# A spectral and mixture-of-experts kernel: column products, gate, spectrum and schedule rearranged

## The chip, the cores and the metric

The kernel runs on one core of one Trainium2 chip. The metric is the device time of one execution in microseconds (us); a comparison takes the median of several executions. TensorE (PE) multiplies matrices into PSUM; VectorE (DVE), ScalarE (ACT) and GpSimd (POOL) work on tiles; SyncE (SP) issues most transfers. Each engine runs its own instructions in order, and engines wait for each other with semaphores. The order within an engine is fixed when the kernel is built, by a scheduler that may move instructions against the order of the Python text.

## The reference: what is computed

The input x has 16 images, 64 channels, 128x128 pixels, float32. Layer 0 is a spectral convolution with a Hartley transform, 20x20 modes, followed by Gaussian blurs over all four axes and a column mask. Layer 1 is a group norm, a Fourier block on 32x32 modes, a second group norm and a mixture of experts:

```
x_ht = dht_2d(x);  out_ht[:, :, :20, :20] = compl_mul2d(x_ht[:, :, :20, :20], w1)
y    = gaussian_smoothing_4d(dht_2d(out_ht) / (H*W)) * mask
h    = afno(group_norm(y)) + y            # afno adds its own input again
feats = gelu(fe_w @ group_norm(h) + fe_b)
out  = sum over 2 shared of gelu(shared_w @ feats + b) / 2
gate_w = softmax of the 4 largest of 16 scores / 2, from the mean of feats
out += sum over experts of gelu(expert_w @ feats + b) * gate_w;   out + h
```

## The kernel before

Everything is float32. The image between the layers is never formed: it stays as 400 mode coefficients, and the pixels are made only once, late.

**Forward stage (L184 to L247), one image after the other.** The image is loaded in four pieces `xt` of 16 channels (1 MB each, five buffers). For each 8 channels, 16 small products with `fwd1` (L202) make a PSUM tile `ps`, which is copied into `t1`, by ScalarE and VectorE in turn (L207, L209). Then 40 column products with `fwd2` (L221) make the 20x20 modes; ScalarE copies half of them to `pn` (L224), VectorE combines them into `xm` (L228 to L231) and adds them, with the weights of the blur over images, into `x2` for up to nine images (L241, L243). When an image of `x2` is complete, VectorE writes a negated and a copied half (L246, L247). With the first eleven images come the weights `wk`: half of them straight, half in reversed order of the second mode, read so from memory (L214).

**Mode mixing (L249 to L285).** For each of 11 rows of modes, 20 products of `wk` with `x2` (L261), copied to `om` by both engines; then a blur over channels (L277) gives `ot`, 400 modes in four chunks of 100 partitions.

**Group norm and mode products (L288 to L448).** `group_norm(h)` runs for two halves of eight images: `dev` products (L340, 4x4), squares on ScalarE (L342), means (L346) and sums (L349), then a chain of VectorE instructions that ends with the scales `s1p`, the shifts `shp` and `sh`. Then for each image, 16 products `psx` with `spec` (L434), scaled by VectorE (L438), and one image-half behind them the first layer of the Fourier block (L419) with a Gelu (L421), written to memory as `o1d`. For ten of the images, `modes` picks 40 coefficients of all images (L401) into `ok`, which goes to memory as `od` and `ond`.

**Stage 5 (L453 to L847), one period per image.** Its constants are loaded first (L463 to L491). The pieces of an image are:

- `spectrum` (L549): loads `s` and the mode part of `bm`.
- `spectrum_f` (twice, L560): second layer of the Fourier block, 64 products into one PSUM tile; VectorE adds the bias `b2` on the way to `bm` (L578) and at the end the shift `sh` (L582).
- `rows` (eight, L588): inverse transform along one axis, `bm` to `u`.
- `pixels` (eight, L613): inverse along the other axis, `u` times `inv2` over 105 rows, copied by ScalarE to `h` (L632), with VectorE's statistics behind it (L636).
- `norm2` (three steps, L645): second group norm, folded into the weights `fs` and a bias.
- `feature` (eight, L677): features, Gelu on ScalarE (L691).
- `gate` (eight steps, L697): small products and activations, the 16 scores ranked on all 128 partitions, and four gathers of expert weights `wl` (L764).
- `group` (48, L812): one product of a tile of features with one shared or chosen expert (L784), Gelu on ScalarE (L789), and VectorE's weighted addition into `h` (L792). After its last one the tile is stored (L803).

All large pieces share three PSUM tiles `pe`. `h` has 14 tiles, eight of them per image, `f` nine, `g` seven. `PIECES` gives each piece its position, counted in groups of its own image; the pieces of all images are sorted by position, so that one image's groups lie beside the preparation of the next:

```
(spectrum_f, (-53, -49)),
(feature, (-9, -9, -8, -7, -6, -6, -3, -1)),
(step("norm", norm2), (-20, -18, -14)),
(step("gate", gate), (2, 3, 4, 6, 7, 7, 8, 10)),
(rows, (-48, -48, -41, -40, -40, -39, -38, -38)),
(pixels, (-36, -33, -28, -24, -24, -24, -24, -24)),
(group, range(NG)),
```

An evacuation by ScalarE is put into its queue one piece later (`on_act`), an addition by VectorE one more after that (`on_dve`).

Of the kernel before, what the change touches and what calls it, by code (L numbers as in the profile page):

```python
# [11 lines left out]
F32 = mybir.dt.float32  # L12
# [17 lines left out]
HR, KC = 52, 105  # L30
CL = C // 2
# [22 lines left out]
def constant_tables():  # L54
# [23 lines left out]
    inv1, inv2 = np.zeros((128, 2, N)), np.zeros((KC, N))  # L78
# [7 lines left out]
    inv1 = inv1.reshape(128, 2, 2, N // 2).transpose(0, 1, 3, 2).reshape(128, 2 * N)  # L86
# [27 lines left out]
    spec = spec.swapaxes(2, 3).reshape(NM, MD * MD) / N  # L114
    spec = np.stack([spec.real, spec.imag], 1)
    dev = np.linalg.qr(dev.reshape(41 * 42, NM), mode="r") / N
# [6 lines left out]
    for loc in range(5):  # L123
# [5 lines left out]
    lower = np.broadcast_to((f_ < e_).reshape(1, NE * NE), (128, NE * NE))  # L129
    ranks = np.broadcast_to(np.repeat(np.arange(TOPK), NE)[None], (128, TOPK * NE))  # L130
# [4 lines left out]
        "inv2": inv2,  # L135
        "spec": chunked(spec.reshape(NM, 2 * MD * MD)),
        "dev": chunked(dev.T.copy()),
        "mean": chunked(np.repeat(mean.reshape(NM, 1), 128, 1)),
        "blurc": blur_matrix(C).T * 2.0 ** -14,
        "sel": sel.reshape(CH, 5 * 32),  # L140
        "grp": grp,
        "lower": lower,
        "ranks": ranks,
        "ident": half[:, None] == np.arange(C)[None, :],
        "eidx": 64 * np.arange(NE)[None, :] + half[:, None],
# [5 lines left out]
def hartley_afno_moe_kernel(ctx: ExitStack, tc: tile.TileContext, a: dict, out: bass.AP):  # L151
# [15 lines left out]
    otp = on_modes.enter_context(tc.tile_pool(name="ot", bufs=1))  # L167
# [4 lines left out]
    sh = const.tile([P, NB, CL], F32, name="sh")  # L172
# [4 lines left out]
    with tc.tile_pool(name="modes", bufs=1) as mp:  # L177
# [6 lines left out]
        with tc.tile_pool(name="f_x", bufs=5) as xp, tc.tile_pool(name="f_t", bufs=2) as tp, \  # L184
# [4 lines left out]
            fwd2 = load(fc, "fwd2", [P, 2 * K, W1], nc.gpsimd)  # L189
            seen = set()  # L190
            for b in range(NB):

                t1 = tp.tile([P, 2 * K, C], F32, name="t1")
                for c0 in range(0, C, 16):
                    xt = xp.tile([P, 16, N], F32, name="xt")
                    nc.sync.dma_start(xt, a["x"][b, :, c0:c0 + 16])
                    for g in range(2):
                        ps = pp1.tile([P, 8, W1], F32, name="ps1")
                        for i in range(8):
                            for h in range(2):  # L200
                                cols = slice(h * 64, (h + 1) * 64)
                                nc.tensor.matmul(ps[cols, i, :], lhsT=xt[:, g * 8 + i, cols],  # L202
                                                 rhs=fwd1, start=True, stop=True)
                        cs = slice(c0 + g * 8, c0 + g * 8 + 8)
                        src = ps[:, :, 0:2 * K].rearrange("p c j -> p j c")
                        if g:
                            nc.vector.tensor_copy(t1[:, :, cs], src)  # L207
                        else:
                            nc.scalar.copy(t1[:, :, cs], src)  # L209
                if b <= K // 2:  # L210
                    nc.sync.dma_start(wk[0:C, b], a["w"][b])
                    kn = (-b) % K
                    nc.sync.dma_start(wk[C:P, b, 0], a["w"][kn, :, 0])
                    nc.sync.dma_start(wk[C:P, b, 1:K], a["w"][kn, :, K - 1:0:-1])  # L214
# [18 lines left out]

                xf = xm.rearrange("p a b -> p (a b)")
                for bo in range(NB):
# [9 lines left out]
                    if not gb[bo, b + 1:].any():  # L245
                        nc.vector.tensor_scalar(x2[0:C, 1, bo], x2[C:P, 0, bo], -1.0, None, ALU.mult)  # L246
                        nc.vector.tensor_copy(x2[C:P, 1, bo], x2[0:C, 0, bo])  # L247

        with tc.tile_pool(name="m_o", bufs=1) as op, \  # L249
                tc.tile_pool(name="m_p", bufs=3, space=PSUM) as pp, \  # L250
                tc.tile_pool(name="m_p2", bufs=2, space=PSUM) as pp2:
            blurc = load(op, "blurc", [C, C], nc.gpsimd)
            om = op.tile([C, NB, NM], F32, name="om")
            omk = om.rearrange("o b (k2 k1) -> o k1 k2 b", k1=K)
            for k1 in range(K // 2 + 1):
# [9 lines left out]
                nc.scalar.copy(omk[:, k1, 0:K:2], lo[:, :, 0])  # L265
                nc.vector.tensor_copy(omk[:, k1, 1:K:2], up[:, :, 0])
                if k1 % (K // 2):
                    nc.scalar.copy(omk[:, K - k1, 0:1], lo[:, 0:1, 1])
                    nc.scalar.copy(omk[:, K - k1, K - 2:0:-2], lo[:, 1:, 1])
                    nc.vector.tensor_copy(omk[:, K - k1, K - 1::-2], up[:, :, 1])  # L270

            for b0 in range(0, NB, 8):
                for ch in range(4):
                    ps = pp2.tile([CH, 8, C], F32, name="pst")
                    for i in range(8):
                        for m0, m1 in ((0, C), (C, CH)):
                            nc.tensor.matmul(ps[m0:m1, i, :],  # L277
                                             lhsT=om[:, b0 + i, ch * CH + m0:ch * CH + m1],
                                             rhs=blurc, start=True, stop=True)
                    dst = ot[:, ch, b0 * C:(b0 + 8) * C]  # L280
                    src = ps.rearrange("p b c -> p (b c)")
                    if ch % 2:
                        nc.scalar.copy(dst, src)
                    else:
                        nc.vector.tensor_copy(dst, src)  # L285


    with tc.tile_pool(name="s_c", bufs=1) as sc, tc.tile_pool(name="s_w", bufs=2) as sw, \  # L288
# [102 lines left out]
        for h in range(2):  # L391
            group_norm(h)
# [525 lines left out]
```

## Time and profile before

| what | value |
|---|---|
| time, median of 3 | 1924.02 us (1912.71 to 1928.27) |
| profiled execution, span | 1919.1 us, clock 0.974 |
| forward stage, to the first mixing product | 268.75 us |
| mixing and channel blur | 268.75 to 294.9 us |
| group norm | 294.96 to 338.03 us |
| mode products and first layer | 338.03 to 496.3 us |
| changeover and first image's preparation | 496.3 to 572.5 us |
| 15 periods of stage 5 | 85.6 us each |

A line of a group or a timeline has the source line, the engine, the operation, what it writes and reads, how often, its busy time and mean, and in brackets or behind the bar the idle time ahead of it with what ended that. A line of the waits has the waiting instruction, the one it waited for, the sum in us, how often, and the longest. `PEld` is the load of weights into TensorE, `SPq` the queue of transfers that SyncE issues. In the line of 40 slices each digit is the busy share in tenths.

### The profile page before, as it was taken

The page shows a single profiled execution, that of the slowest core. Times are in us where ns is not written, and L with a number is a line of the kernel's source. Part 1 is how long each engine was busy: PE and PEld are TensorE (multiplying, and loading weights), DVE is VectorE, ACT ScalarE, POOL GpSimd, SP SyncE. Part 2 cuts the span into 40 slices and gives each one's busy share as a digit, 9 for nine tenths or more (in the row PEclk, how much of TensorE's full clock was granted, in tenths as well). Part 3 has the DMA queues.
Part 4 walks back from the last instruction along what each step waited for, and adds up shares of the span by engine and source line. Part 5 has one row for each costly group of instructions (what it writes and reads, how often), then busy time and mean ns, then how long its engine had stood idle before and what let it go on. Part 6 is the DMA issues. An engine that isn't in the chain of part 4 may idle for free.

```text
span 1919.1 us, 55574 instructions
## 1 busy us (share of the span) xinstructions
PE 1735.4 (90%) x24568; PEld 946.2 (49%) x24568; DVE 1399.6 (73%) x1999; ACT 1278.1 (67%) x1542; POOL 146.4 (8%) x143
## 2 busy tenths in 40 slices
PE   6776779999689999999999999999999999999987
PEld 6676774332355454454635454454535445453521
DVE  2354653421139898988889898988989898888988
ACT  1111121112258888888888988888888888888896
POOL 0000000003001011010101001010101101010110
PEclk9899999999889999999999999999999999999998
DMA  9999823014312223222321223223222322222023
GB/s 331 310 303 299 291 73 96 33 56 124 92 21 35 79 55 70 67 47 68 67 78 35 80 56 68 67 46 89 47 78 38 84 54 63 67 51 74 26 67 90
DMA packets 140626, 181.15 MB, mean 94 GB/s; under 512 B 107456, under 2 KB 108709, under 8 KB 131965
## 3 DMA queue, kind: packets, MB, share of 16 engines
q1 hardware_dynamic: 136512, 170.55, 32.1%
q0 software_dynamic: 3872, 7.04, 1.5%
q8 instruction: 193, 3.16, 0.7%
q14 instruction: 49, 0.39, 0.1%
HBM read 98.51 MB, written 79.04 MB: 93 GB/s over the span
## 4 chain that ended last, share of the span: by engine, by line
PE 45%; ACT 18%; DVE 17%; issue 15%; DMA 3%; SPq 1%; DVEq 0%; POOL 0%; ACTq 0%; POOLq 0%
PE pe L784 10%; DVE h L792 9%; ACT g L789 9%; PE pe L624 9%; PE psx L434 6%; PE ps L202 6%; PE pe L602 4%; ACT f L691 4%; PE ps L221 2%; DVE stats L636 2%; ACT u L607 2%; DVE bm L578 2%; PE pso L419 2%; PE psd L340 2%; DMA xt<-in_x_dram 2%
## 5 line engine op out<-in xcount | busy, mean ns | idle before, releaser
L792 DVE SCALAR_TENSOR_TENSOR h<-g,wt,h 128x1024 f32<-128x1024 f32 x512 | 623.9, 1278 | 59.7 <-ACT g L789 59.7
L789 ACT ACTIVATE g<-pe,wl 128x1024 f32<-128x1024 f32 x512 | 541.2, 1142 | 41.9 <-PE pe L784 40.4
L784 PE MATMUL pe<-f,wl 64*64 64x512 f32 x4096 | 492.8, 602 | 3.9 <-DMA wl<-exd,ati 3.6
L792 DVE SCALAR_TENSOR_TENSOR h<-g,h 128x1024 f32<-128x1024 f32 x256 | 302.7, 1219 | 52.7 <-ACT g L789 52.2
L789 ACT ACTIVATE g<-pe,vec_sb 128x1024 f32<-128x1024 f32 x256 | 279.6, 1134 | 7.5 <-PE pe L784 4.2
L784 PEld LDWEIGHTS pe<-f,wl 64*64 64x64 f32 x4096 | 137.9, 132 | 275.0 <-ACT g L789 119.6
L784 PE MATMUL pe<-f,shw 64*64 64x512 f32 x2048 | 259.9, 602 | 0.0
L624 PEld LDWEIGHTS pe<-inv_sb,u 105*128 105x128 f32 x2048 | 234.9, 193 | 50.4 <-ACT g L789 36.5
L624 PE MATMUL pe<-inv_sb,u 105*128 105x128 f32 x2048 | 246.5, 279 | 1.4 <-ACT u L607 1.4
L202 PE MATMUL ps<-fwd_sb,xt 128*64 128x64 f32 x4096 | 144.3, 237 | 52.7 <-issue 38.0
L636 DVE BATCH_NORM_STATS2 stats<-h 128x6 f32<-128x512 f32 x256 | 162.6, 683 | 35.1 <-ACT h L632 34.5
L632 ACT COPY h<-pe 128x1024 f32<-128x1024 f32 x128 | 129.6, 1012 | 78.2 <-PE pe L624 69.0
L691 ACT ACTIVATE f<-pe,fb 128x1024 f32<-128x1024 f32 x128 | 148.0, 1184 | 35.0 <-PE pe L687 35.0
L202 PEld LDWEIGHTS ps<-fwd_sb,xt 128*64 128x64 f32 x4096 | 139.6, 152 | 56.0 <-issue 44.1
L687 PE MATMUL pe<-h,fs 64*64 64x512 f32 x1024 | 140.9, 622 | 13.6 <-DVE bm L582 11.8
L607 ACT COPY u<-pe 105x1024 f32<-105x1024 f32 x128 | 125.5, 1033 | 36.2 <-PE pe L602 36.2
L602 PEld LDWEIGHTS pe<-inv_sb,bm 64*64 64x64 f32 (+1 forms) x4096 | 119.2, 123 | 53.3 <-PE pe L784 20.5
L602 PE MATMUL pe<-inv_sb,bm 64*64 64x128 f32 (+1 forms) x4096 | 135.2, 271 | 10.5 <-DVE gs L702 8.6
L209 ACT COPY t<-ps 128x320 f32<-128x320 f32 x64 | 27.3, 426 | 148.2 <-PE ps L202 148.2
L434 PE MATMUL psx<-spec_sb,ot 100*64 100x512 f32 x512 | 116.7, 598 | 0.0
L421 ACT ACTIVATE o<-pso,b 128x512 f32<-128x512 f32 x32 | 22.0, 687 | 121.5 <-PE pso L419 121.5
L784 PEld LDWEIGHTS pe<-f,shw 64*64 64x64 f32 x2048 | 67.7, 132 | 55.9 <-issue 22.5
(160 smaller groups left out, 1250.7 us busy)
## 6 DMA issues: line engine op xcount, KB each, us to landing
xt<-in_x_dram SPq DMA_DIRECT2D x64, 1024.0 KB
out_dram<-h SPq DMA_DIRECT2D x256, 256.0 KB
o1d<-o SPq DMA_DIRECT2D x16, 512.0 KB
s<-o1d SPq DMA_DIRECT2D x16, 512.0 KB
bm<-od SPq DMA_DIRECT2D x96, 50.0 KB
wk<-in_w_dram SPq DMA_DIRECT2D x11, 320.0 KB
wk<-in_w_dram SPq DMA_DIRECT2D x11, 304.0 KB
spec_sb<-in_spec_dram SPq DMA_DIRECT2D x1, 3200.0 KB
```

Source lines behind the costliest of these rows:

```text
L202: nc.tensor.matmul(ps[cols, i, :], lhsT=xt[:, g * 8 + i, cols], rhs=fwd1, start=True, stop=True)
L434: nc.tensor.matmul(ps[ri * C:(ri + 1) * C], lhsT=ot[:, kc, b * C:(b + 1) * C], rhs=spec[:, kc, ri * 1024 + n * 512:ri * 1024 + (n + 1) * 512],
L602: nc.tensor.matmul(ps[cs, h, i, :], lhsT=bm[rs, 4 * q + i, cs], rhs=inv1[rs, part], start=True, stop=True)
L607: nc.scalar.copy(dst.rearrange("p h s n -> p n h s"), ps[0:KC].rearrange("p h s n -> p n h s"))
L624: nc.tensor.matmul(ps[:, r // 4, r % 4 * N:(r % 4 + 1) * N], lhsT=box["u"][0:KC, 2 * row:2 * row + 2, :].rearrange("p h c -> p (h c)"), rh ...
L632: nc.scalar.copy(h, ps)
L636: nc.vector.bn_stats(box["stats"][:, 2 * t + p, :], h[:, p])
L687: nc.tensor.matmul(ps[p * C:(p + 1) * C, half], lhsT=box["fs"][rows_], rhs=box["h"][t][rows_, p], start=True, stop=True)
L691: nc.scalar.activation(f, ps, AF.Gelu, bias=box["fb"], accum_out=box["sums"][:, t:t + 1])
L784: nc.tensor.matmul(ps[half * C:(half + 1) * C, p], lhsT=w[rows_], rhs=f[rows_, half], start=True, stop=True)
L789: nc.scalar.activation(g, ps, AF.Gelu, bias=bias)
L792: nc.vector.scalar_tensor_tensor(h, g, share(), h, ALU.mult, ALU.add)
```

## The change

The change touches every stage.

- Forward: the column products are written one image behind the row products, all copies of `ps` are made by ScalarE, the negated half of `x2` too; the reversed half of `wk` is loaded straight into `wn` and reversed by ScalarE.
- Mixing: `om` is laid out over 128 partitions, the channel blur uses both row halves of the array, and four PSUM tiles.
- Constants are loaded earlier, on the other side of the memory, beside mixing and the mode products.
- Group norm: both halves side by side on 64 partitions each, `dev` as an upper triangle (10 products for 16), and the results as one small tile `gs1`.
- First layer: two products of 64 columns for one of 128.
- Bias and shift: the bias `b2` of the spectrum becomes two more rows of `u` and `inv2` (107 for 105), made once; the shift is the bias of ScalarE's copy to `h`. So the spectrum is copied by ScalarE, plainly, and VectorE leaves it.
- Gate: the 16 experts lie on 16 partitions; ranks and picks are 16x16, and a product with ones spreads the result over 128 partitions.
- Schedule: new positions.

```diff
+            wn = fc.tile([P, K, C], F32, name="wn")
+            def along_columns(b, t1):          # L221 to L247 of before
...
-                        nc.vector.tensor_scalar(x2[0:C, 1, bo], x2[C:P, 0, bo], -1.0, None, ALU.mult)
+                        nc.scalar.mul(x2[0:C, 1, bo], x2[C:P, 0, bo], -1.0)
...
-                        if g:
-                            nc.vector.tensor_copy(t1[:, :, cs], src)
-                        else:
-                            nc.scalar.copy(t1[:, :, cs], src)
+                        nc.scalar.copy(t1[:, :, cs], src)
+                    if c0 == 0 and behind:
+                        along_columns(*behind)
+                behind = (b, t1)
+                if 0 < b <= K // 2 + 1:
+                    k = b - 1
+                    nc.scalar.copy(wk[C:P, k, 0], wn[C:P, 0])
+                    nc.scalar.copy(wk[C:P, k, 1:K], wn[C:P, K - 1:0:-1])
                 if b <= K // 2:
                     nc.sync.dma_start(wk[0:C, b], a["w"][b])
-                    nc.sync.dma_start(wk[C:P, b, 0], a["w"][kn, :, 0])
-                    nc.sync.dma_start(wk[C:P, b, 1:K], a["w"][kn, :, K - 1:0:-1])
+                    nc.sync.dma_start(wn[C:P], a["w"][(-b) % K])
...
-            om = op.tile([C, NB, NM], F32, name="om")
+            om = op.tile([P, NB, NM // 2], F32, name="om")
...
+                    pq = [pp2.tile([CH, 8, C], F32, name="pst") for h in range(2)]
                     for i in range(8):
+                        for h, (m0, m1) in ((0, (0, C)), (1, (C, CH)), (1, (0, C)), (0, (C, CH))):
...
+        for g, cols in halves:
+            for rc in range(4):
+                for kc in range(rc, 4):
+                    nc.tensor.matmul(ps[:CH], lhsT=dev[:, kc, rc * CH:(rc + 1) * CH],
+                                     rhs=ot[:, kc, cols], start=(kc == rc), stop=(kc == 3))
...
-            nc.tensor.matmul(ps, lhsT=wc.rearrange("p r c -> p (r c)"), rhs=xk[:, cols],
-                             start=True, stop=True)
+            for ri in range(2):
+                nc.tensor.matmul(ps[ri * C:(ri + 1) * C], lhsT=wc[:, ri], rhs=xk[:, cols],
+                                 start=True, stop=True)
...
+            if b == HB:
+                bn1s, bn1f, bn2s, bn2f = prepare()
...
+        u = up_.tile([P, N, C], F32, name="u")
+        nc.sync.dma_start(u[KC:KU], b2x)
...
-                for i in (0, 8):
-                    j = q * 16 + i
-                    nc.vector.tensor_tensor(bmf[:, :, :, j:j + 8],
-                                            ps[:, i:i + 8].rearrange("p i r c -> p r c i"),
-                                            b2.unsqueeze(3).to_broadcast([P, 2, CL, 8]), ALU.add)
+                nc.scalar.copy(bmf[:, :, :, q * 16:(q + 1) * 16], ps.rearrange("p i r c -> p r c i"))
                 if q:
-                    nc.vector.scalar_tensor_tensor(bm[0:C + 1, :, 0], sh[0:C + 1, box["b"]], float(N),
-                                                   bm[0:C + 1, :, 0], ALU.mult, ALU.add)
...
-                    lhsT=box["u"][0:KC, 2 * row:2 * row + 2, :].rearrange("p h c -> p (h c)"),
+                    lhsT=u[0:KU, 2 * row:2 * row + 2, :].rearrange("p h c -> p (h c)"),
...
-                nc.scalar.copy(h, ps)
+                nc.scalar.activation(h, ps, AF.Identity, bias=gs1[:, 1, box["b"]:box["b"] + 1])
...
-            h2 = smp.tile([C, P], F32, name="h2")
+            h2 = smp.tile([C, NE], F32, name="h2")
...
-            nc.vector.tensor_tensor(gt, s_f, s_e, ALU.is_gt)
-            nc.vector.tensor_tensor(eq, s_f, s_e, ALU.is_equal)
-            nc.vector.tensor_tensor(eq, eq, lower, ALU.mult)
-            nc.vector.tensor_tensor(gt, gt, eq, ALU.add)
+            nc.vector.tensor_tensor(tmp, sco, pick[:, NE:2 * NE], ALU.mult)
+            nc.vector.tensor_reduce(own, tmp, AX.X, ALU.add)
+            nc.vector.scalar_tensor_tensor(tmp, sco, own, pick[:, 0:NE], ALU.is_equal, ALU.mult)
+            nc.vector.scalar_tensor_tensor(tmp, sco, own, tmp, ALU.is_gt, ALU.add)
...
+            nc.tensor.matmul(z[:, 0:2 * TOPK], lhsT=ones_e, rhs=oh.rearrange("p i k -> p (i k)"),
+                             start=True, stop=True)
...
-            (spectrum_f, (-53, -49)),
-            (feature, (-9, -9, -8, -7, -6, -6, -3, -1)),
-            (step("norm", norm2), (-20, -18, -14)),
-            (step("gate", gate), (2, 3, 4, 6, 7, 7, 8, 10)),
-            (rows, (-48, -48, -41, -40, -40, -39, -38, -38)),
-            (pixels, (-36, -33, -28, -24, -24, -24, -24, -24)),
+            (spectrum_f, (-57, -50)),
+            (feature, (-5, -4, -3, -2, -2, -2, -2, 0)),
+            (step("norm", norm2), (-19, -16, -10)),
+            (step("gate", gate), (2, 3, 5, 7, 8, 8, 10, 12)),
+            (rows, (-50, -49, -48, -48, -48, -40, -39, -38)),
+            (pixels, (-36, -32, -28, -24, -24, -24, -23, -23)),
```

## The prediction

> **What bounds the kernel now.** First the page's engine shares and the span in 40 slices (48 us each), to see that the kernel has stages with different limits.
>
> ```profile
> PE 1735.4 (90%) x24568; PEld 946.2 (49%) x24568; DVE 1399.6 (73%) x1999; ACT 1278.1 (67%) x1542; POOL 146.4 (8%) x143
> DMA  9999823014312223222321223223222322222023
> GB/s 331 310 303 299 291 73 96 33 56 124 92 21 35 79 55 70 67 47 68 67 78 35 80 56 68 67 46 89 47 78 38 84 54 63 67 51 74 26 67 90
> ```
>
> The DMA engines are full for five slices: the forward transform, 0 to about 260 us, moves x (64 loads of 1 MB). After that DMA is mostly idle. So the forward stage is read by transfers, the rest by engines. The waits of the DMA queue within 0 to 250 us say what holds the next load back:
>
> ```profile
> SPq L196 <- PE ps L202: 170.0, 50, 9.7
> ```
>
> The loads wait for TensorE to free one of five xt buffers. Both holds are close together: the last 20 loads (no w among them) are issued over 70.9 us, 14.2 us an image, while the DMA share in 180 to 250 us is only 0.83. There TensorE itself waits for VectorE's copies of ps (9.5 us of idle ahead of L221, 4 ahead of L202, each with more before it).
>
> Next the chain of waits between the forward stage and stage 5 (the per-image pipeline). Group norm is a serial run on TensorE:
>
> ```profile
> 294.96 15.60 PE psd L340 x32
> 310.57 3.43 PE psd L346 x8
> 314.00 3.43 PE psd L349 x8
> 317.43 13.73 PE psd L340 x32
> ```
>
> with a second 3.43 + 3.43 behind it: 43.1 us up to the first psx at 338.03. Then the mode products (L434, L419) keep TensorE busy to 496.3 us. The changeover to stage 5:
>
> ```profile
> 496.34 0.70 ACT o L421
> ...
> 509.17 3.56 DMA bm<-od
> ...
> 512.77 6.09 PE pe L569 x256
> ```
>
> 16.5 us from the last product to the first of stage 5; in between the queue issues some 20 constants one by one, and s and bm are behind them.
>
> Stage 5 is 15 equal periods and a tail. One period, as a window:
>
> ```profile
> 1131.20:1216.80 85.60, 82.03 (x1112) 42.12 (x1108) 74.99 (x97) 74.88 (x86) 7.20 (x6) 1.00 0.26 63
> ```
>
> (columns: TensorE, weight load, VectorE, ScalarE, GpSimd, clock, DMA.) No engine fills 85.6 us, so I ask who waits, in 960 to 1302 us (four periods):
>
> ```profile
> ACT h L632 <- PE pe L624: 14.9, 28, 0.8
> ...
> PEld pa L659 <- DVE n L656: 9.0, 4, 2.4
> ...
> ACT h L632 <- DMA out_dram<-h: 3.5, 4, 1.6
> PE pe L687 <- DVE bm L582: 3.4, 4, 0.8
> ```
>
> ScalarE never waits for VectorE; all its 10.6 us of idle an image are waits for TensorE, and once for a store. Its timeline shows where:
>
> ```profile
> 967.38 4.13 ACT L789 ACTIVATE g<-pe,wl 128x1024 f32<-128x1024 f32 x4 [1.33 <-PE pe L784]
> ...
> 991.09 1.11 ACT L691 ACTIVATE f<-pe,fb 128x1024 f32<-128x1024 f32 x1 [0.66 <-PE pe L687]
> ...
> 995.76 1.11 ACT L691 ACTIVATE f<-pe,fb 128x1024 f32<-128x1024 f32 x1 [1.45 <-PE pe L687]
> ...
> 1043.30 1.01 ACT L632 COPY h<-pe 128x1024 f32<-128x1024 f32 x1 [1.58 <-DMA out_dram<-h]
> ```
>
> So the stage is a two-server line, TensorE then ScalarE, with three PSUM tiles between; VectorE hurts only where TensorE waits for it (the norm's small product, and PSUM tiles that VectorE empties).
>
> **What the Trainium skill says.** "Perfetto Trace Analysis", Optimization Strategy: a kernel may have regimes with different most-contended engines, and interleaving them may help. The trace agrees: five pixel tiles in a row take TensorE 9.14 us (1.83 each) against ScalarE's 0.92 spacing, groups alone 0.89 (4.45 us for five) against 1.02 (6.14 for six). "TensorE: Matmul & The Clock Gate", Part 3 (Packing small matmuls): products on different tiles of the array run concurrently. The trace agrees: 8 psx products in two column halves take 3.58 us, 0.45 each, and a 100-column psd product 0.86 (13.73/16). "DMA: Bandwidth & Descriptors", Specifications: below 512 B a transfer does not reach line rate. w's reversed half has 256 B runs; no row prices it alone. "ScalarE: Activation LUTs", Rules: 0.3 us + 0.83 ns an element, so 1.15 us for 1024 as an estimate; L789 shows 1.14.
>
> **The change, part by part.**
>
> Forward. All 128 ps copies go to ScalarE: 8 x 0.43 + pn 0.33 + reversed w copies about 1.4 (1216 elements; L409 took 1.20) + a sign change 0.36 = 5.5 us of an image of 12 or more: hidden. VectorE loses 4 x 0.49. TensorE then no longer waits behind VectorE's 3 us of accumulation: per image 8 ps tiles x 0.96 + 2.55 + two waits of 0.7 = 11.6 us. In the compiled order L212 of an image still stands before the next image's first product, so "one behind" itself I cost at nothing. An image then needs its transfer, 11.8 us (14.2 x 0.83), say 12.8: 5 x 1.4 = 7 us. The w images last 15.0 ((172-7)/11); their 0.64 MB cost 3.2 of it beside the 11.8 of x, 1.8 at x's rate (4.2 MB in 11.8), so contiguous loads save up to 1.5, I take 1.0: 11 us. Added wait: the load of wn waits on the queue for ScalarE's reversed copy, and the next x loads are behind it. The compiled order puts that copy after the previous image's last ps copy, some 7 us after the wn load comes up, with four x loads (12 us) still under way; so no gap. Sum -18 (-5 to -32). The sign changes leave VectorE's tail: -2.
>
> Mixing and pst. The 440 psm instructions stay (13.7 us at 0.031). pst's products now use both row halves and four PSUM tiles: 8.4 + 1.4 us become 5 to 8; but v2's copies stand between ScalarE's pst copies and wait for v2's load, queued behind 5 MB of constants. I take -3 (0 to -6).
>
> Group norm. dev triangular: 20 products for 32, 20 x 0.86 = 17.2. mean and ones on 64 columns in halves: 8 pairs at 0.9 = 7.2. Plus 0.8 for the last square: 25 for 43, -18. VectorE's chain behind psv is now exposed: reduce 0.69, root 0.4, reciprocal 0.55, some eighteen small ones, 6.5 to 7; TensorE has two psx tiles, 7.2 us, to do meanwhile. Range -13 to -19.
>
> Mode products. L419 as two column halves: 0.9 for 1.06, 32 times; half of it taken, -3. prepare() puts 13 small ScalarE copies (about 3 us) beside an engine 15% busy: nothing.
>
> Changeover. Constants and bm are loaded during the mode products. What is left: Gelu 0.7, write of o1d and landing about 3.7, s issued and landed about 4: 8.4 for 16.5, and VectorE's 1.3 + 0.2 for spectrum becomes about 2 on ScalarE. -8, and -1 for image 1's spectrum. Range -5 to -12.
>
> Stage 5, per image. ScalarE gains 2 spectrum tiles at 1.03 (L607, the nearest strided copy; the skill's estimate 1.15 is the upper end), loses 0.2 with the 16-wide h2. h with a bias becomes an activation (+0.1 each, the difference of spacing), in pixel stretches where TensorE limits. VectorE loses 4 x 0.64 + 0.2 and in the gate 3.7 becomes about 1.9. It then waits for GpSimd's pow behind the first gather, about 2.4 instead of 1.05. Behind that wait are h additions, and for them g tiles (seven) wait: no one else. The ones product adds 0.3 to TensorE; the gathers start about 5 us before group 16 needs them. Now stretches, TensorE against ScalarE (group or feature 0.89, row 1.0, pixel 1.83, spectrum 1.95; group 1.02, feature 1.09, copies 0.92):
> before: groups 0-11 with 8 rows and gate 20.6 / 20.8; 12-23 with 3 pixels 16.2 / 15.0; 5 pixels and 2 groups 10.9 / 6.6; 26-38 12.6 / 13.5; 39-47 with 8 features and 2 spectrum tiles 19.0 / 17.9. The larger ones sum to 80.4; measured 85.6, so 5.2 are stalls.
> after: 19.5 / 19.8; 16.2 / 15.3; 10.9 / 6.8; 26-42 with one spectrum tile 18.1 / 18.5; 43-47 with 7 features, one spectrum tile, 2 rows 14.6 / 15.6: 81.0.
> Of the stalls, the norm's shrinks by 1.0 (three groups instead of two between its steps), the store's by 1.0 (the last two pixel tiles come a group later), the PSUM tile held by VectorE (0.84) goes: 2.4 stay. Period 83.4, -2.2, over 15 periods -33. Ends: 81.0 (-69) and stalls unchanged, 86.2 (+9). The tail (48 additions of 1.2 to 1.28) is VectorE's and stays.
>
> Sum: -18 - 2 - 3 - 18 - 3 - 9 - 33 = -86: 1838 us.
>
> **Rivals.**
> (1) ScalarE takes over stage 5: its 2.1 us more do not fit into its waits, and the period stays at 85.6 to 86.2. For: after the change ScalarE is the larger in three stretches of five. Against: 3.9 us of its idle lie right beside the spectrum tiles. Only the front gains, -53 + 0 to 9: 1871 to 1880.
> (2) Stalls vanish: period near 81, 1924 - 53 - 69 = 1802. For: all four named stalls are touched. Against: pixel tiles still come three and two together.
> (3) Slower: the wn load drains the queue, about 5 us in each of 10 images, +50 - 11, and ScalarE's 2.7 us come on top of the period, +40; the rest saves 35: 1968. Against: the compiled order of the reversed copy, and the idle above.
>
> **How the numbers follow.** Forecast 0.60, (1) 0.20, (2) 0.15, (3) 0.05. Forward without gain is within the range of each. 1790 leaves out the best half of (2); 1890 holds (1) with a weaker front. Faster by over 1% (under 1905) 0.92, within 0.05, slower 0.03.
>
> **What would show it.** Last x load issued near 225 us rather than 242.9; psd to first psx 25 us; last L501 to first L622 about 9 us; period 83.4 with ScalarE near 77 busy, no TensorE wait for VectorE's bm, the norm wait under 0.5 and the store wait under 1. Wrong if SPq waits for ScalarE with DMA idle, if features make TensorE wait ahead of the gate, or if ScalarE's idle does not fall.

## The result, and the profile after

The changed kernel takes 1863.91 us (median; 1857.94 to 1870.27) against 1924.92 us (1912.71 to 1928.27): ratio 0.9695, 95% interval 0.9641 to 0.9748. It is faster by 61 us where 86 were forecast. The experiments below are one execution each, except e_best1 with six; four executions of one kernel spread over 12 us (changed) and 16 us (before), so a stretch is read from its run's profile, and whole times only roughly. The profiled executions differ by 58.6 us (1919.1 and 1860.5), which the stages divide so:

| stage, from and to | before | after | change | predicted |
|---|---|---|---|---|
| forward, to the first mixing product | 268.75 | 261.05 | -7.7 | -20 |
| mixing and blur, to the first group-norm product | 26.2 | 35.6 | +9.4 | -3 |
| group norm, to the first psx of the mode products | 43.1 | 24.5 | -18.6 | -18 |
| mode products, to the last product | 158.3 | 150.7 | -7.6 | -3 |
| changeover and first preparation, to the first expert's Gelu | 76.2 | 64.1 | -12.1 | -9 |
| stage 5: 15 periods and the tail | 1346.6 | 1324.5 | -22.1 | -33 |

First the page: engine shares, and the 40 slices, now 46.5 us each.

```profile
PE 1698.4 (91%) x24644; PEld 935.0 (50%) x24644; DVE 1277.5 (69%) x1790; ACT 1367.7 (74%) x1674; POOL 120.9 (6%) x140
DMA  9999842114212222322232322322232322222023
GB/s 339 318 313 299 308 138 52 46 59 136 69 24 64 53 81 47 93 36 81 54 72 55 64 81 41 96 38 81 47 78 50 70 72 45 73 56 70 27 71 92
```

ScalarE has gained 89.6 us and VectorE lost 122, as intended. In the sixth slice (233 to 279 us) there are now 138 GB/s where the kernel before had 73 in its own (240 to 288 us): the constants come beside the mixing.

The queue's waits within 0 to 250 us:

```profile
SPq L245 <- PE ps L251: 150.2, 49, 8.8
SPq L267 <- ACT wk L264: 35.0, 10, 5.6
```

The 170 us of before have become 150, and a new wait of 35 stands beside them, of the load of `wn` for ScalarE's reversed copy.

Group norm, by TensorE's timeline (start, busy time, instruction):

```profile
296.67 3.69 PE L397 MATMUL psd<-ot,mean_sb 100*64 100x512 f32 x16
300.29 17.48 PE L406 MATMUL psx<-ot,dev_sb 100*100 100x512 f32 x40
317.70 3.65 PE L412 MATMUL psd<-sq,ones 100*64 100x512 f32 x16
321.19 7.04 PE L548 MATMUL psx<-spec_sb,ot 100*64 100x512 f32 x32
```

One such run replaces the two of before. A stretch of the mode products, by the same view, before and after:

```profile
388.16 3.65 PE L434 MATMUL psx<-spec_sb,ot 100*64 100x512 f32 x16
...
396.39 1.12 PE L419 MATMUL pso<-xk,wc 128*128 128x512 f32 x2
397.44 1.07 PE L401 MATMUL psd<-ot,sel_sb 100*32 100x256 f32 x16
398.44 3.65 PE L434 MATMUL psx<-spec_sb,ot 100*64 100x512 f32 x16
```

```profile
389.22 3.65 PE L548 MATMUL psx<-spec_sb,ot 100*64 100x512 f32 x16
...
397.00 1.03 PE L499 MATMUL pso<-xk,wc 128*64 128x512 f32 x4
397.96 1.07 PE L480 MATMUL psd<-ot,sel_sb 100*32 100x256 f32 x16
398.96 3.65 PE L548 MATMUL psx<-spec_sb,ot 100*64 100x512 f32 x16
```

Between the first and the last line lie two groups of psx with their first-layer products, and one selection: 10.28 us before, 9.74 after, so 0.27 less for each group. The changeover, by the timeline of all engines:

```profile
471.99 0.69 ACT L501 ACTIVATE o<-pso,b 128x512 f32<-128x512 f32 x1 [0.42 <-PE pso L499]
...
475.42 0.80 SPq L606 DMA_DIRECT2D s<-o1d  x2
...
478.94 0.28 PE L622 MATMUL pe<-v2a,s 128*32 128x64 f32 x1 [6.99 <-DMA s<-o1d]
```

From the last Gelu of the layer to the first product of stage 5 there are now 6.95 us, for 16.4. A period of stage 5 is counted from the first expert's Gelu of one image to that of the next; the first five take 84.07 us each, and 85.6 before. A window of four times 84.07 us (columns as before: TensorE, weight load, VectorE, ScalarE, GpSimd, clock, DMA share, GB/s), and the waits in 960 to 1302 us. The last line is of the kernel before: the second part of its norm wait, of which the prediction shows the first (9.0).

```profile
956.36:1292.64 336.28, 326.89 (x4430) 169.35 (x4426) 281.25 (x356) 309.26 (x350) 22.18 (x24) 1.00 0.27 65
```

```profile
ACT h L677 <- PE pe L669: 14.1, 27, 0.7
...
PEld pa L704 <- DVE n L701: 6.7, 4, 1.7
...
ACT h L677 <- DMA out_dram<-h: 4.7, 5, 1.0
...
PE pa L704 <- DVE n L701: 3.2, 4, 0.8
```

```profile
PE pa L659 <- DVE n L656: 5.4, 4, 1.5
```

ScalarE is busy for 309.26 / 4 = 77.3 us a period. TensorE's wait for VectorE's `bm` is gone. The norm's wait is 9.9 / 4 = 2.5 us an image (before 14.4 / 4 = 3.6). The store's wait is not smaller: over all 16 images it sums to 20.1 us, and to 9.2 before, where it came in one image of three. It does not come evenly: the first fourteen periods run from 83.6 to 86.8 us, with a mean of 84.30 (before 85.5 to 85.9, mean 85.62). So the first five show the changed kernel a little better than it is.

### The profile page after: what moved, and what is told of

Same layout as the page of the kernel before. It is cut to its first block, busy times and chain, and to the rows that moved or that the text cites. A ratio compares the mean times of both kernels' runs of the same rounds, so it can differ in the third digit from the quotient of the medians.

```text
span 1860.5 us, 55630 instructions
## 1 busy us (share of the span) xinstructions
PE 1698.4 (91%) x24644; PEld 935.0 (50%) x24644; DVE 1277.5 (69%) x1790; ACT 1367.7 (74%) x1674; POOL 120.9 (6%) x140
## 3 DMA queue, kind: packets, MB, share of 16 engines
q8 instruction: 193, 3.16, 0.7%
## 5 line engine op out<-in xcount | busy, mean ns | idle before, releaser
L669 PEld LDWEIGHTS pe<-inv_sb,u 107*128 107x128 f32 x2048 | 234.4, 192 | 62.3 <-ACT g L831 36.5
L826 PE MATMUL pe<-f,shw 64*64 64x512 f32 x2048 | 251.2, 600 | 0.0
L669 PE MATMUL pe<-inv_sb,u 107*128 107x128 f32 x2048 | 248.8, 279 | 1.2 <-ACT u L652 1.2
L677 ACT ACTIVATE h<-pe,gs 128x1024 f32<-128x1024 f32 x128 | 142.7, 1115 | 80.6 <-PE pe L669 60.5
L647 PE MATMUL pe<-inv_sb,bm 64*64 64x128 f32 (+1 forms) x4096 | 143.2, 273 | 1.4 <-ACT bm L629 1.2
L255 ACT COPY t<-ps 128x320 f32<-128x320 f32 x128 | 53.4, 424 | 121.1 <-PE ps L251 121.1
L732 PE MATMUL pe<-h,fs 64*64 64x512 f32 x1024 | 134.0, 610 | 1.6 <-DVE n L709 1.6
L219 DVE TENSOR_TENSOR xm<-ps,pn 64x20 f32<-64x20 f32 x32 | 5.5, 171 | 168.2 <-ACT pn L215 168.0
L806 POOL DMA_INDIRECT wl<-exd,ati x64 | 66.8, 1045 | 702.5 <-ACT g L831 610.6
```

The lines of the kernel that those rows point to most:

```text
L647: nc.tensor.matmul(ps[cs, h, i, :], lhsT=bm[rs, 4 * q + i, cs], rhs=inv1[rs, part], start=True, stop=True)
L669: nc.tensor.matmul(ps[:, r // 4, r % 4 * N:(r % 4 + 1) * N], lhsT=u[0:KU, 2 * row:2 * row + 2, :].rearrange("p h c -> p (h c)"), rhs=inv2, ...
L677: nc.scalar.activation(h, ps, AF.Identity, bias=gs1[:, 1, box["b"]:box["b"] + 1])
L732: nc.tensor.matmul(ps[p * C:(p + 1) * C, half], lhsT=box["fs"][rows_], rhs=box["h"][t][rows_, p], start=True, stop=True)
L826: nc.tensor.matmul(ps[half * C:(half + 1) * C, p], lhsT=w[rows_], rhs=f[rows_, half], start=True, stop=True)
```

## The mixing: two causes

Theory 1: two PSUM tiles in place of three make TensorE wait for the copies of the tile before. Theory 2: the loads, now beside the mixing, hold up TensorE's supply of instructions. TensorE's timeline of the changed kernel has both signs (in brackets the idle time ahead and what ended it; "issue" is idle time that no semaphore explains):

```profile
261.05 5.84 PE L294 MATMUL psm<-x,wk 128*64 128x64 f32 x120 [6.80 <-DVE ones L376]
267.72 1.39 PE L294 MATMUL psm<-x,wk 128*64 128x64 f32 x40 [0.83 <-DVE om L303]
270.29 1.40 PE L294 MATMUL psm<-x,wk 128*64 128x64 f32 x40 [1.18 <-DVE om L303]
...
280.05 1.75 PE L294 MATMUL psm<-x,wk 128*64 128x64 f32 x51 [1.87 <-issue]
282.75 2.60 PE L294 MATMUL psm<-x,wk 128*64 128x64 f32 x76 [0.94 <-DVE om L303]
288.86 0.34 PE L294 MATMUL psm<-x,wk 128*64 128x64 f32 x4 [3.52 <-issue]
```

The kernel before did the 440 products in one run:

```profile
268.75 14.93 PE L261 MATMUL psm<-x,wk 128*64 128x64 f32 x440 [8.79 <-DVE x L247]
```

**e_psum3.**

```diff
-                tc.tile_pool(name="m_p", bufs=2, space=PSUM) as pp, \
-                tc.tile_pool(name="m_p2", bufs=4, space=PSUM) as pp2:
+                tc.tile_pool(name="m_p", bufs=3, space=PSUM) as pp, \
+                tc.tile_pool(name="m_p2", bufs=2, space=PSUM) as pp2:
```

> The mixing gets three PSUM tiles again, as in the kernel before, and the products with blurc behind it two in place of four; nothing else moves. From the first mixing product to the first group-norm product the changed kernel took 35.6 us (kernel before: 26.2), where I had expected a few us less than before. Theory 1 (two PSUM tiles let TensorE wait for the copies of the tile before, whose ScalarE-VectorE chain is longer than TensorE's work on a tile): the stretch falls to 27 to 30 us and TensorE's waits for om go to nearly nothing. Theory 2 (the constants' loads, now issued as the mixing starts, hold up TensorE's instruction fetch): the stretch stays within 2 us of 35.6, gaps of 1 us and more inside a tile with no semaphore behind them stay, and the waits for om alone go.

The waits for `om` fall from 4.3 to 1.7 us, but the idle "issue" time grows from 5.4 to 7.4:

```profile
275.48 4.00 PE L294 MATMUL psm<-x,wk 128*64 128x64 f32 x126 [2.40 <-issue]
284.49 0.38 PE L294 MATMUL psm<-x,wk 128*64 128x64 f32 x4 [5.00 <-issue]
```

The mixing itself takes 26.0 us for 28.7, and the way to the first psx of the mode products 61.0 for 60.1: up to there nothing is gained, as theory 2 has it. The stretch that the expectation named came to 31.2 us, in neither band; the scheduler puts some group-norm products among the blur's here and in e_psum3_late, so it cuts across work, and psx is the better mark. The edit also leaves the blur two PSUM tiles for four.

**e_late.**

```diff
-        dev = load(sc, "dev", [CH, 4, NM])
...
-        spec = load(sc, "spec", [CH, 4, 2 * MD * MD])
-        exw = load(sc, "exw", [P, C, NE])
...
+            def after_mixing(name, shape):
+                t = sc.tile(shape, F32, name=name + "_sb", tag=name)
+                nc.vector.tensor_copy(t[0:1, 0, 0:1], om[0:1, NB - 1, 10:11])
+                nc.vector.tensor_copy(t[0:1, 0, 0:1], om[C:C + 1, NB - 1, 10:11])
+                nc.sync.dma_start(t, a[name].rearrange("p (a b) -> p a b", b=shape[2]))
...
```

The two small copies read the last rows of `om`, so each of the three loads waits for the mixing's last copies.

> The three large constants (dev, spec, exw) are asked for only once the mixing's last copy is done, in place of before the mixing; PSUM tiles stay at two. Theory 1 (two PSUM tiles): the stretch from the first mixing product to the first group-norm product stays above 30 us. Theory 2 (loads beside the mixing hold up TensorE's instruction fetch): the gaps inside tiles without a semaphore, some 5.4 us in all, go, and the stretch falls by 5 us or more, to 30 us or less. The group norm behind it may then wait some us for dev; that is read apart and is no part of either theory.

The gaps without a semaphore are gone from the mixing, and a regular wait for the tile before is left, 0.8 us in every 3.5:

```profile
269.88 2.72 PE L291 MATMUL psm<-x,wk 128*64 128x64 f32 x80 [0.79 <-DVE om L300]
273.40 2.72 PE L291 MATMUL psm<-x,wk 128*64 128x64 f32 x80 [0.80 <-DVE om L300]
...
289.82 0.48 PE L320 MATMUL pst<-blurc_sb,om 64*36 64x64 f32 x5 [2.93 <-issue]
```

The mixing takes 21.1 us. But the last line shows such a gap again, in the blur, where the loads now run; the stretch to the group norm is 31.1 us, 4.5 less and still in theory 1's band, and psx comes at 58.2 us. Each theory names something real, and neither is enough.

**e_psum3_late**, both edits together.

> Both: three PSUM tiles for the mixing and the three large constants asked for after it. If the two causes add, the stretch from the first mixing product to the first group-norm product comes to 22 to 26 us, so at or below the kernel before's 26.2; if one of them alone is the cause, it is within 1 us of the better of the two single runs; if neither is, it stays near 35.

```profile
258.46 16.16 PE L291 MATMUL psm<-x,wk 128*64 128x64 f32 x440 [6.81 <-DVE ones L384]
```

One run of 440 products again.

| kernel | mixing, to the first blur product | of it waits for `om` | of it "issue" | first mixing product to first psx | GB/s beside the mixing |
|---|---|---|---|---|---|
| before | 16.3 | 0 | 0 | 69.2 (old group norm) | 7 |
| changed | 28.7 | 4.3 | 5.4 | 60.1 | 170 |
| e_psum3 | 26.0 | 1.7 | 7.4 | 61.0 | 178 |
| e_late | 21.1 | 3.4 | 0 | 58.2 | 23 |
| e_psum3_late | 17.1 | 0 | 0 | 50.8 | 29 |

Within the mixing the two edits nearly add: 2.7 and 7.6 us alone, 11.6 together. Up to psx they bring 9.3 us together, and -0.9 and 2.0 alone, because the stretch between the mixing and psx takes some of it back: 31.5 us as changed, 35.0 in e_psum3, whose blur has fewer tiles, 37.1 in e_late, whose loads run beside the blur, 33.8 with both. The seven kernels below that leave the mixing as changed need 58.8 to 60.1 us to psx, so each edit alone stays within 1 us of that spread; the two that have both edits need 51.3 and 52.8. The stretch that the expectation named is 21.1 us with both, below the 22 to 26 of causes that add. The kernel as a whole took 1853.37 us.

On what "issue" is, the Trainium skill ("Runtime: NRT & Kernel Launch", Instruction fetch mechanics) says that an engine refills its instruction memory in blocks of 16 KiB by transfers of its own, mostly hidden. The queue line of the changed kernel's profile agrees on the block, 3.16 MB / 193 = 16.4 KB:

```profile
q8 instruction: 193, 3.16, 0.7%
```

It does not agree on the hiding: gaps of 1.87 to 5.00 us appear where bulk loads run and go with them. The single transfers in the trace show that these gaps are late refills. In the changed kernel, up to the end of the mixing, TensorE has 29 gaps named "issue", 57.6 us in all, and every one of them ends 1.28 to 1.60 us after a transfer of 16,384 bytes has landed on this queue; only 5% of TensorE's products start at such a distance from a landing. The two gaps of the mixing end at 280.05 and 288.86, and the transfers landed at 278.57 and 287.33. A refill itself takes no longer beside the loads (1.0 to 1.2 us in this mixing, 0.9 to 1.3 in the kernel before, where three of them landed and left no gap), so it comes late rather than slowly. That the loads make it late is what e_late and e_psum3_late show for the mixing; where it waits, no run shows.

## The forward stage: bound by TensorE and its gaps

The forecast took transfers for the bound. TensorE's waits up to the first mixing product, of the kernel before and then of the changed one, say otherwise:

```profile
PE ps L202 <- issue: 38.0, 18, 4.3
PE ps L221 <- issue: 11.4, 6, 3.2
PE ps L221 <- DVE t L207: 9.5, 14, 0.7
...
PE ps L202 <- DVE t L207: 3.9, 3, 2.0
PE ps L202 <- DMA xt<-in_x_dram: 3.3, 3, 2.5
```

```profile
PE ps L251 <- issue: 44.9, 21, 5.9
...
PE ps L212 <- ACT t L255: 8.3, 16, 0.5
...
PE ps L212 <- issue: 7.3, 6, 1.9
...
PE ps L251 <- DMA xt<-in_x_dram: 4.6, 4, 2.1
```

TensorE hardly waits for an image tile (3.3 and 4.6 us); it is the loads that wait for TensorE. The account closes: busy 186.4 to 181.7 (-4.7), waits for copies 13.4 to 8.3 (-5.1), issue 49.4 to 52.2 (+2.8), tiles +1.3, the last wait for `x2` 8.8 to 6.8 (-2.0): -7.7. VectorE's copies did leave, and ScalarE's copy of the fourth piece took over most of the wait. The gaps, over 3 us an image, were on the page, and the forecast left them out. They are 27 of the 29 late refills counted above, so the transfers may still set this pace, by another way than the image tiles. No run takes loads out of this stage to test that; in stage 5, beside 65 GB/s, such gaps sum to 1.2 us.

Nine runs with the forward stage as changed start the mixing at 256.7 to 263.8 us, mean 260.5; an edit has to leave that spread to be seen.

**e_wn2**: two buffers for the plain copy.

```diff
-            wn = fc.tile([P, K, C], F32, name="wn")
+            wns = [fc.tile([P, K, C], F32, name=f"wn{i}") for i in range(2)]
...
-                    nc.sync.dma_start(wn[C:P], a["w"][(-b) % K])
+                    nc.sync.dma_start(wns[b % 2][C:P], a["w"][(-b) % K])
```

> The plain copy of the other half of w lands in two buffers in turn, in place of one, so that its load no longer waits in the SP queue for ScalarE's reversed copy of the one before (35.0 us of such waits in the changed kernel). Theory A (the wait keeps the transfers of the forward stage behind it idle, and these set its end): the last image tile is asked for 5 to 10 us earlier than at 237 us, and the mixing starts as much earlier than at 261.05 us. Theory B (the queue runs ahead of the transfers, which are the bound, so the wait costs little): the last image tile within 2 us of 237 us, the mixing's start within 2 us of 261.

The mixing starts at 266.14 us; the wait for ScalarE is gone from the queue, and the wait for TensorE has taken its place:

```profile
SPq L245 <- PE ps L251: 187.5, 58, 8.9
```

187.5 for 150.2 + 35.0: nothing behind the queue had been starved. The last image tile is asked for at 239.5 us (changed: 237.0), so it is neither earlier, as theory A had it, nor within theory B's 2 us; that the mixing starts 2.4 us beyond the spread is one run, unexplained.

**e_nobehind**: the column products after their own image.

```diff
-                    if c0 == 0 and behind:
-                        along_columns(*behind)
-                behind = (b, t1)
                 fwd2 = fwd2 or load(fc, "fwd2", [P, 2 * K, W1])
+                along_columns(b, t1)
...
-            along_columns(*behind)
```

> The column products are put back where the kernel before had them, after the image's own fourth tile in place of one image behind; all else is as changed. The four unedited or hardly edited runs so far start the mixing at 258.5 to 261.1 us and ask for the last image tile at 234 to 237 us. Theory A (transfers bound the forward stage, and the delay of the column products only took idle time that the transfers cover anyway): the mixing starts at most 3 us later than 261 us, within the spread of those runs. Theory B (my prediction's: ScalarE's and VectorE's copies of an image, held up by the column products, held up the image tiles): the start moves back by 5 us or more, to 266 us or later, toward the kernel before's 268.75 us.

260.86 us: the part that gives the change its name brings nothing that can be seen.

**e_oldw**: the reversed half read in 256-byte runs again.

```diff
...
-                    nc.sync.dma_start(wn[C:P], a["w"][(-b) % K])
+                    kn = (-b) % K
+                    nc.sync.dma_start(wk[C:P, b, 0], a["w"][kn, :, 0])
+                    nc.sync.dma_start(wk[C:P, b, 1:K], a["w"][kn, :, K - 1:0:-1])
```

> The reversed half of w is read from memory in the order in which it is used again, in runs of 256 bytes, and ScalarE's reversed copy falls away; all else is as changed. My prediction counted on 11 us of transfers saved by the plain load, nine images with w at about 1 us each and some of the queue's waits. Theory A (that was the forward stage's gain): the mixing starts at 269 us or later. Theory B (the short packets cost the transfers nearly nothing: the kernel before took 15.0 us an image with w, the changed one 14.8): it starts within 3 us of 261 us, and may even start earlier, as the 35 us of waits of the SP queue for the reversed copy go.

268.67 us, just under theory A's mark, 4.9 beyond the spread and 8.2 above its mean. But only 4.6 of the 8.2 arise while images with `w` are loaded: the last twenty image loads, which have no `w` among them, begin at 174.8 us here and at 166.0 to 173.2 (mean 170.2) in the nine runs. So the plain load is worth something, and one run does not size it. TensorE waited not for tiles but at "issue": 48.0 + 9.8 = 57.8 us, more than in any other run (47.2 to 54.4).

**e_altcopy**: the copies of `ps` by both engines in turn.

```diff
-                        nc.scalar.copy(t1[:, :, cs], src)
+                        if g:
+                            nc.vector.tensor_copy(t1[:, :, cs], src)
+                        else:
+                            nc.scalar.copy(t1[:, :, cs], src)
```

> The copies of the forward stage's PSUM tiles alternate between ScalarE and VectorE again, as in the kernel before; the load of w and the place of the column products stay as changed. The mixing has started at 256.7 to 261.1 us in the seven runs that leave the forward stage as changed or put only the column products back. Theory A (my prediction's: VectorE's accumulation kept its share of the copies, and so the image tiles, late; 1.4 us an image in the last five, 7 us in all): it starts at 265 us or later. Theory B (transfers set the pace and the copies' engine doesn't matter): 257 to 262 us.

266.13 us, as theory A has it, but not by its mechanism: the waits for the copies are 9.5 us for 8.3, while TensorE's busy time is 185.9 for 181.7, a size that runs with unedited copies also show (180.8 to 186.2), and 2.7 us are a wait for the load of `fwd2`. What the copies' engine is worth, from 1 to 5 us, stays open.

## Stage 5: the copy and the positions belong together

**e_oldsched**: the positions of before, except the gate's.

```diff
-            (spectrum_f, (-57, -50)),
-            (feature, (-5, -4, -3, -2, -2, -2, -2, 0)),
-            (step("norm", norm2), (-19, -16, -10)),
+            (spectrum_f, (-53, -49)),
+            (feature, (-9, -9, -8, -7, -6, -6, -3, -1)),
+            (step("norm", norm2), (-20, -18, -14)),
...
-            (rows, (-50, -49, -48, -48, -48, -40, -39, -38)),
-            (pixels, (-36, -32, -28, -24, -24, -24, -23, -23)),
+            (rows, (-48, -48, -41, -40, -40, -39, -38, -38)),
+            (pixels, (-36, -33, -28, -24, -24, -24, -24, -24)),
```

> Stage 5 gets the kernel before's positions for the spectrum's copies, the gate's feature, the norm's step, the rows and the pixels; what the steps do stays as changed. Period of an image in stage 5: 85.57 us before, 84.07 us changed. Theory A (the schedule brings the larger share): 85 us or more. Theory B (the removed waits, by the bias in the columns' inverse and the spectrum's copy on ScalarE, bring it and the schedule little): 84.5 us or less.

**e_dvespec**: the copy on VectorE.

```diff
-                nc.scalar.copy(bmf[:, :, :, q * 16:(q + 1) * 16], ps.rearrange("p i r c -> p r c i"))
+                for i in (0, 8):
+                    j = q * 16 + i
+                    nc.vector.tensor_copy(bmf[:, :, :, j:j + 8],
+                                          ps[:, i:i + 8].rearrange("p i r c -> p r c i"))
```

> The spectrum's plain copy out of PSUM goes to VectorE, in two halves of 8 rows as in the kernel before, in place of one ScalarE copy; the bias stays in the columns' inverse and the schedule as changed. ScalarE loses some 2.1 us of work an image, VectorE gains about as much. Theory A (ScalarE is the bound and its copy costs its own length): the period falls from 84.07 to 82 to 82.7 us. Theory B (TensorE waits for VectorE's late copy again, and ScalarE for TensorE): it stays at 84 us or rises to 85.5 us, with TensorE's wait for bm by VectorE back.

**e_dvespec_oldsched**: both.

> Both edits of stage 5 that were undone one by one: the spectrum's copy on VectorE in halves, and the kernel before's positions. Alone, the positions gave a period of 84.73 us and VectorE's copy 91.47 us, against 84.07 us changed and 85.57 us before. Theory A (the new positions are only good with the copy on ScalarE; with VectorE's they put the rows' products right behind a copy that is late): the period falls back to 85 to 86.5 us. Theory B (a copy on VectorE costs some 7 us an image wherever it stands, and the kernel before was spared that by something else): 91 us or more.

The periods, each the mean of the first five, and in brackets the mean of all fourteen before the last:

| us | new positions | positions of before |
|---|---|---|
| copy by ScalarE | 84.07 (84.30) | 84.73 (84.47) |
| copy by VectorE | 91.47 (91.43) | 86.39 (86.89) |

(The kernel before: 85.6 (85.62).) With the copy on ScalarE the positions bring 0.66 us in the first five, between the two expectations, but only 0.2 over the fourteen, in theory B's band; with it on VectorE the same positions cost 5.1 (4.5). The copy on ScalarE brings 1.7 us (2.4) at the old positions and 7.4 (7.1) at the new ones. So what the new positions are worth by themselves is small; that they do not bear a late copy is clear. Of the expectations, e_dvespec's 91.47 lies beyond both, and e_dvespec_oldsched's 86.39 is theory A's. The timelines of VectorE and TensorE in e_dvespec show why:

```profile
1049.46 9.65 DVE L837 SCALAR_TENSOR_TENSOR h<-g,wt,h 128x1024 f32<-128x1024 f32 x8
1059.03 1.28 DVE L631 COPY bm<-pe 128x512 f32<-128x512 f32 x2
```

```profile
1060.46 3.69 PE L829 MATMUL pe<-f,wl 64*64 64x512 f32 x16 [4.91 <-DVE bm L631]
```

The copy takes 1.28 us, but eight additions stand ahead of it on VectorE, and TensorE waits 4.91 us for the PSUM tile. What ScalarE pays for the copy, 2.1 us an image, fits into its idle time; what TensorE pays for VectorE's late one does not. From before to e_dvespec_oldsched the period rises by 0.8 us (1.3), though copy and positions are those of before. The bias on ScalarE's copy of `h` is as large, 8 x (1115 - 1012 ns), but the gate and the two further rows changed too, so this is not separated.

**e_best0**: the mixing of e_psum3_late, norm and pixels moved.

```diff
-            (step("norm", norm2), (-19, -16, -10)),
+            (step("norm", norm2), (-17, -13, -8)),
...
-            (pixels, (-36, -32, -28, -24, -24, -24, -23, -23)),
+            (pixels, (-36, -32, -28, -25, -24, -23, -22, -21)),
```

> Three PSUM tiles and late constants in the mixing (50.8 us from the first mixing product to the first psx of the mode products, against 60.1 us changed), and in stage 5 the norm's steps at -17, -13, -8 and the pixels at -36, -32, -28, -25, -24, -23, -22, -21. Theory A (the store's wait of 1.0 us, the norm's of 2.5 us and the pixel copies' waits of some 3 us an image are due to the positions): the period falls from 84.07 us to 82 to 83.3 us, and the time to about 1830 to 1845 us. Theory B (a wait that goes at one place comes back at the next, since TensorE's and ScalarE's work of 81 to 82 us leaves little): the period within 0.4 us of 84.07 us, the time near 1853 us.

84.32 us a period and 1859.07 us: theory B. The store's wait is gone, and the spread pixels wait for TensorE instead: within 900 to 1240 us, 18.1 us for 14.0.

```profile
ACT h L685 <- PE pe L677: 18.1, 26, 0.8
```

**e_best1**: the same mixing, the norm alone moved.

> Three PSUM tiles and late constants in the mixing, the pixels' positions as changed, and of the schedule only the norm's steps at -17, -13, -8. With pixels and norm moved together the norm's and the store's waits went, yet the period was 84.32 us, with the pixel copies' waits for TensorE larger by 1 us an image. Theory A (TensorE's norm wait of 2.5 us an image is on the path in part; the spread pixels alone took the gain back): the period falls to 83 to 83.7 us and the time to 1838 to 1848 us. Theory B (the norm's wait lies beside ScalarE's own work and costs nothing): 84.0 to 84.3 us, and 1850 to 1858 us, which is the mixing's 9 us below the changed kernel. Ratio to the kernel before: A 0.953 to 0.960, B 0.960 to 0.966.

The period is 83.69 us, as theory A has it, the time 1852.24 us (1843.75 to 1862.38) against 1933.68 beside it: ratio 0.9592 (0.9563 to 0.9621), below the changed kernel's 0.9695. The norm's wait within 900 to 1240 us is (4.5 + 0.8) / 4 = 1.3 us an image for 2.5:

```profile
PEld pa L712 <- DVE n L709: 4.5, 4, 1.3
...
PE pa L712 <- DVE n L709: 0.8, 3, 0.4
```

Over the fourteen periods it is 83.81 us, for 84.35 in e_psum3_late with the same mixing, so the norm's positions bring 0.5 us. The ratio lies at the edge of theory A's band (0.953 to 0.960), the time itself in theory B's (1850 to 1858): the kernel before took 1933.68 us beside it, 9 more than beside the changed kernel.

## Why the prediction was right and where it was wrong

- **Group norm** (-18, measured -18.6): right by its own count of products. VectorE's chain behind it held TensorE up for only 0.5 us (ahead of L499).
- **Forward** (-18 and -2, measured -7.7): the 2 us came, as the last wait for `x2` went from 8.8 to 6.8. The 18 did not: "An image then needs its transfer, 11.8 us" put the pace at the transfers of x, for which TensorE hardly waits (4.6 us in all). From its first product to that last wait TensorE takes 246.9 us, 15.4 an image: 11.4 busy, 3.3 of "issue" gaps (52.2 / 16), which the forecast put at nothing, 0.5 of waits for copies and 0.3 for image tiles. The images with `w` gained 2.3 us where 11 were forecast (the last twenty image loads begin at 170.1 us for 172.4), and those twenty loads 3.7 where 7 were (67.2 us for 70.9). The last one is issued at 237.0 us, not 225. Costing "one behind" at nothing was right, and so was rejecting a queue that runs dry.
- **Mixing** (-3, measured +9.4): the blur shrank from 9.8 to 6.9 us as forecast. "The 440 psm instructions stay" was the failed step: their number stayed, their PSUM tiles and the traffic beside them did not, and 16.3 us became 28.7. The result lies outside the stated 0 to -6.
- **Mode products** (-3, measured -7.6): right mechanism; the term was 0.16 us for each of 32 groups, 5.1 in all, and was then halved without a reason from the profile. The runs show 0.27 a group, 8.6 in all. The Trainium skill ("TensorE: Matmul & The Clock Gate", Part 3) has such products on different tiles run concurrently, and the trace agrees: in the two timelines of the result, four products of 64 columns take 1.03 us, two of 128 columns 1.12.
- **Changeover** (-9, measured -12.1, just past its range of -5 to -12): right in kind; the write of `o1d` and the load of `s`, with the Gelu, took 6.95 us where 8.4 were allowed, and the first image's preparation behind them 2.6 us less than before rather than 1.
- **Stage 5** (-2.2 a period, measured -1.5 in the first five, -1.3 in the fourteen): ScalarE's 77 us were right (77.3), and so was the end of the PSUM wait. The norm's stall shrank by 1.1 as the sum has it, but not to the "under 0.5" that the list of signs asked: three additions (3.61 us on VectorE) still stand ahead of its step. The store's wait, forecast to shrink by 1.0, went from 0.6 to 1.3 us an image (9.2 and 20.1 over 16); that is the term that failed. The rival of a ScalarE-bound period (85.6 to 86.2) did not come: the period is 84.1, with ScalarE idle for 6.8 of it.

The forecast's terms that failed, 12 us each in forward and mixing and 11 in stage 5, were offset in part by 8 more in mode products and changeover. So the right total owes something to luck: 1864 lies nearer to the 1871 of rival (1) than to 1838, and it is stage 5's period, not the total, that tells the two apart.

## What to carry to other kernels

Count idle time that no semaphore explains as part of an engine's work: here over 3 us an image set the pace of a stage that looked bound by transfers. When loads are moved earlier, look at which engine issues thousands of small instructions beside them, and when buffers are regrouped, at the copies that free them; a gain in one stretch can be paid back in the next, so measure both, and try two edits together before dropping either. Where an evacuation moves between engines, look at its queue position on the new engine before its duration: here a copy of 1.3 us made TensorE wait 4.9.

## What the runs showed of the hardware

- Bulk loads of 170 to 178 GB/s beside 440 small products gave TensorE gaps of 1.87 to 5.00 us each, 5.4 to 7.4 us in all (two runs); at 7 to 29 GB/s there were none (three runs).
- Each of the 29 gaps of this kind up to the end of the changed kernel's mixing ended 1.28 to 1.60 us after a 16,384-byte transfer of instructions had landed; in the mixing, the transfers took 1.0 to 1.2 us beside the loads and 0.9 to 1.3 us, in the kernel before, without them.
- An unedited forward stage varied by 7 us between runs, with TensorE's busy time (180.8 to 186.2 us) moving as well.
- ScalarE's copy of 1024 elements from PSUM takes 1012 ns (the kernel before), with a bias for each partition 1115 ns (the changed one).
